# A transformer block with attention and two chosen experts: curve in pieces, row sums in DRAM, maxima turned on VectorE, and another order at both ends

## The chip, the cores and the metric

The kernel runs on one core of a Trainium2 chip. The metric is the device time of one execution in microseconds (us), as the median of several runs; smaller is better. Single instructions are read from one profiled execution.

## The reference

The input x has 4 sequences of 2048 tokens with 512 numbers each, all in float32. The block adds three things:

```python
xn = _layernorm(x, axis=-1)
x = x + attention(xn) + ffn(xn)
# attention: 16 heads of 32; softmax(q k^T / sqrt(32)) v, then a projection with bias
# ffn: per sequence, the first token chooses the 2 best of 8 experts;
#      sum over both of (gelu(xn W1 + b1) W2 + b2), divided by 2
```

The Gelu is the exact one (approximate=False). Each softmax subtracts the row's maximum.

## The kernel before, in words

**Units of work.** `B` is 4 sequences, `DC` 4 groups of 4 heads (a group fills the 128 partitions, 32 for each head), `NCH` 4 chunks of `CH` = 512 queries, `NT` 16 tiles of 128 keys. A unit is one step of one key tile for one chunk and group; there are 4 × 4 × 4 × 16 = 1024, and the loop at L829 goes through them with `U`, beginning `LEAD` = 22 steps early, at U = -22.

**A step.** Attention is done in two passes, and each step does one part of each. The first pass, 22 steps ahead, multiplies queries with keys only to find the maxima (`score_max`, L706, four matmuls m, each reduced by VectorE at L855). The second pass makes the scores again with the keys on the partitions: `shift` (L720) first writes the negated maxima into four PSUM banks s by a bf16 matmul of `ones_b` with `negm`, `score` (L729) adds the products, and ScalarE takes the exponential of each bank into p (L849). On even steps `weigh` (L738) multiplies two p tiles by v, into a ninth bank, acc. All tiles of a step come from one ring of eight PSUM banks (`bank`, L277), in the order in which the code asks for them. p has four buffers.

**The softmax sums.** GpSimd adds the 16 p tiles of a chunk into `psum` (`add_weights`, L756); the last tile is added by an accumulating DMA that GpSimd issues (L764). In the next chunk matmuls with `ones` sum over the keys (`add_keys`, L768, key step 4 or 5), VectorE takes reciprocals in four pieces (L870), GpSimd multiplies (`divide`, L816, key step 12 or 14), and the result goes to DRAM. In the last chunk of all no additions are made on GpSimd: `add_last` (L786) sums pairs of p tiles by matmuls.

**The maxima as shifts.** At the end of a chunk's first pass (key step 9 of the chunk before its own) VectorE reduces to the negated maxima, `neg` (L794). One step on, GpSimd splits them into three bf16 parts (`rest`, L796, casts at L799). Three steps after that `turn_maxima` (L805) transposes the parts by four TensorE transposes (L809) and VectorE copies them to `negm` (L812).

**Dense work.** On odd steps `dense` (L585) takes one item of a plan (`Plan`, L38): projections to q, k and v for the group or sequence to come, the first expert layer (w1, in seven products `STEPS` of block-combined operands, grouped in `GAPS`), the second (w2) or the output projection (proj). `Plan` gives the fixed items their slots, fills the others in order, and leaves some slots empty ("rests", at key step 5); it moves a rest away from the slot in which a curve is due (`curve`, L147). It also says at which step each load is issued: up to eight steps before its first use, in order on SP's queue (`loads`, L218).

**The curve.** Once the product (3, 1) or (2, 1) of a w1 part is in, half of the hidden tile, 128 × 2048, is complete. It is put down for two steps later (`curves`, L625 to L627). There ScalarE applies Gelu at L853, behind the step's four exponentials. In such a step `dense` leaves combining to VectorE. ScalarE's functions live in tables, which an instruction of their own loads: Gelu, exp and the square root each need another.

**Rows.** A w2 item adds its product to a row tile (L633), which goes through `part_dram`. For the first expert the row is loaded from x, and four steps later GpSimd adds the sequence's bias to it (L881): `bias` holds the mean of both experts' b2 plus the projection's bias (`load_bias`, `sum_bias`, L647 to L664).

**Normalisation.** Of the later sequences it is spread over the steps. The square root of all variances (`root`, L431) comes in one step of each of these sequences: VectorE adds epsilon (L433), ScalarE takes the root (L434), VectorE the reciprocal, GpSimd the rest.

**Both ends.** Before the loop the first sequence is normalised, turned and projected chunk by chunk (L666 to L689): statistics, root and normalisation of chunk c + 1 are issued behind the turning of chunk c, then K and Q of chunk c. Ahead of it the routing (L459 to L478) chooses the experts. After the loop (L944 on) come the last weighing and sums, the projection of the last chunk but one (`last2`, L952), three quarters of the last chunk's (`last1`, L960), and the last quarter piece by piece: reciprocal, product, matmul (L967), addition, store.

**Queues.** DMAs are issued by SP in program order, apart from the accumulating ones on GpSimd's. A DMA waits on SP for its data or its buffer, and what stands behind it waits too. `later(u, ...)` puts an issue down for the end of step u.

Of the kernel before, what the change touches and what calls it, by code (L numbers as in the profile page):

```python
# [37 lines left out]
class Plan:  # L38
# [6 lines left out]
    def __init__(self, B, DC, NCH, NT, TPC):  # L45
# [193 lines left out]
def block_kernel(  # L239
# [44 lines left out]
    xn_dram, t_dram, v_dram, att_dram, part_dram, ws_dram = {}, {}, {}, {}, {}, {}  # L284
    for b in range(B):
        for k in range(TOP_K):
            ws_dram[b, k] = tc.dram_tile([P, DC, D], F32, name=f"ws_dram_{b}_{k}")
    wqk_dram = [tc.dram_tile([P, DC, D], F32, name=f"wqk_dram_{n}") for n in range(2)]
    for b in range(B):
        for c in range(NCH):  # L290
            xn_dram[b, c] = tc.dram_tile([P, DC, CH], F32, name=f"xn_dram_{b}_{c}")
            v_dram[b, c] = tc.dram_tile([P, TPC, D], F32, name=f"v_dram_{b}_{c}")
            att_dram[b, c] = tc.dram_tile([P, DC, CH], F32, name=f"att_dram_{b}_{c}")
            t_dram[b, c] = tc.dram_tile([P, DC, CH], F32, name=f"t_dram_{b}_{c}")
            for i in range(TPC):
                part_dram[b, c, i] = tc.dram_tile([P, D], F32, name=f"part_dram_{b}_{c}_{i}")
# [45 lines left out]
    def load(tag, key):  # L342
# [30 lines left out]
        elif tag == "row":  # L373
            b, c, k, i = key
            src = part_dram[b, c, i] if k else x[b, c * CH + i * P : c * CH + (i + 1) * P, :]
# [11 lines left out]
    nc.gpsimd.memset(ones, 1.0)  # L387
    ones_b = const.tile([P, P], BF16, name="ones_b")
    nc.gpsimd.memset(ones_b, 1.0)


    spread = []
# [10 lines left out]
    nc.sync.dma_start(x_first[0], x_rows(0, 0))  # L403
# [27 lines left out]
    def root(mv, sd, nb, a, z, np_=P):  # L431

        nc.vector.tensor_scalar(sd[:np_, a:z], mv[:np_, a:z, 1], EPS, None, ALU.add)  # L433
        nc.scalar.activation(sd[:np_, a:z], sd[:np_, a:z], AF.Sqrt)  # L434
# [147 lines left out]

    outs = {}

    def dense(item, U, on_dve, between):  # L585
# [79 lines left out]


    mv, sd, nb = stat_tiles(0)

    def first_norm(c):
        for i in range(TPC):  # L670
            stats(mv, c * TPC + i, x_first[c][:, i, :])
        root(mv, sd, nb, c * TPC, (c + 1) * TPC)
# [3 lines left out]
    first_norm(0)  # L676
    for c in range(NCH):
# [108 lines left out]
    def add_last(u):  # L786
        add_keys(
            place(u)[:3], bank(f"keys_{u}"), [pT[u], pT[u + 1]], u > plan.units - NT
        )

    def split(where, n):

        neg = small.tile([P, GH, TPC], F32, tag="neg", name="neg_%d_%d_%d" % where)
        nc.vector.tensor_reduce(neg, mx[where], AX.X, ALU.min)  # L794

        def rest():  # L796
            s = spread[n % 2].rearrange("p i j d -> p j i d")
            for part in range(3):
                nc.gpsimd.tensor_copy(s[:, :, :, part], neg)  # L799
                if part < 2:  # L800
                    nc.gpsimd.tensor_tensor(neg, neg, s[:, :, :, part], ALU.subtract)

        return rest

    def turn_maxima(where, n):  # L805
        negm[where] = small.tile([P, CH], BF16, tag="negm", name="negm_%d_%d_%d" % where)
        pt = ps.tile([P, CH], BF16, tag="bank", name="mt_%d_%d_%d" % where)
        for i in range(TPC):
            nc.tensor.transpose(  # L809
                pt[:, ts(i, P)], spread[n % 2][:, i].rearrange("p j d -> p (j d)"), ident_b  # L810
            )
        nc.vector.tensor_copy(negm[where], pt)  # L812
# [6 lines left out]

    loads = plan.loads(BUFS, -LEAD - 1)  # L820
# [6 lines left out]
    row_ready = {}  # L827

    for U in range(-LEAD, plan.units):  # L829
# [21 lines left out]
        if curve is not None:  # L851
            flat = curve.rearrange("p f n -> p (f n)")
            nc.scalar.activation(flat, flat, AF.Gelu)  # L853
        for dst, t in maxima:
# [25 lines left out]
        for t, key in row_ready.pop(U, []):  # L880
            nc.gpsimd.tensor_tensor(t, t, bias[key[0]], ALU.add)  # L881
        if second:
            add_weights(U)

# [10 lines left out]
        for step, sb, n in plan.extra.get(U, []):  # L895
# [6 lines left out]
            elif step == "root":  # L902
                root(*norms[sb], 0, NT)
            elif step == "normal":
# [7 lines left out]
        if last % NT == 3 and NT < last <= plan.units + 3:  # L912
            turn_maxima(*pending[1:3])
# [6 lines left out]
        for s, tag, key in loads.get(U, []):  # L920
            t = load(tag, key)
            if tag == "row" and key[2] == 0:
                row_ready.setdefault(U + 4, []).append((t, key))
# [22 lines left out]
    add_last(U - 2)  # L946
    where = place(U - 1)[:3]
    w = held["wb", ("proj",)]
    for i in range(TPC):
        pp = bank(f"last2_{i}")  # L950
        for g in range(DC):
            nc.tensor.matmul(  # L952
                pp, ends[2][:, g, ts(i, P)], w[:, g, :], start=(g == 0), stop=(g == DC - 1)
            )
        finish(B - 1, NCH - 2, i, pp, ends[3][:, i, :], U)
# [7 lines left out]
    for i in range(TPC):  # L963
        q = ts(i, P)
        nc.vector.reciprocal(sums[where][:, q], sums[where][:, q])  # L965
        nc.vector.tensor_tensor(att[where][:, q], sacc[where][:, q], sums[where][:, q], ALU.mult)  # L966
        nc.tensor.matmul(  # L967
            tail[i], att[where][:, ts(i, P)], w[:, DC - 1, :], start=False, stop=True
        )
# [47 lines left out]
```

## Time and profile before

| What | Value |
|---|---|
| median of 3 runs | 5042.79 us (5037.69 to 5044.59) |
| the profiled execution | 5042.55 us |
| its span in the profile | 5040.8 us |
| mean granted TensorE clock | 0.997 |
| Gelu on 128 × 2048 (L853) | 32 times, 1912 ns |
| exponential on 128 × 512 (L849) | 4096 times, 603 ns |
| addition to psum on GpSimd (L766) | 819 times, 4545 ns |
| mean busy share of the DMA engines | a third, 113 GB/s |

A group's line gives source line, engine, operation, output and inputs, shape, count, then busy time in us, the mean in ns, and the engine's idle time just before it with what ended that. A line of the waits gives who waited, for whom, the total in us, how often and the longest. A timeline's line gives start and length in us, and in brackets the engine's idle time before. PE is TensorE, PEld its weight load, ACT ScalarE, DVE VectorE, POOL GpSimd, SP the engine that issues DMAs. The profiled execution is 1.75 us longer than its span.

### The profile page before, as it was taken

The numbers are of one execution on the slowest core, as the hardware profiler recorded it, in microseconds if no ns is written. First come the engines' busy times: TensorE is split into PE (matmuls) and PEld (weight loads), VectorE is DVE, ScalarE is ACT, GpSimd is POOL, SyncE is SP. The second block draws the span as 40 slices with busy tenths as digits, with TensorE's granted clock in tenths as the row PEclk, the third lists the DMA queues.
The fourth block names the chain that finished last, engine by engine and source line by source line (L and its number), as shares of the span: only waits on it lengthen the run. The fifth ranks groups of instructions, "written<-read, shape, count | busy, mean of one in ns | idle before, by whom it ended". The sixth has DMA issues, their size and how long they took to land. (4 is left out here: it accounts for less than half of the span.)

```text
span 5040.8 us, 107883 instructions
## 1 busy us (share of the span) xinstructions
PE 4947.0 (98%) x45028; PEld 1725.8 (34%) x45028; DVE 3740.2 (74%) x5909; ACT 2394.0 (47%) x4406; POOL 4429.2 (88%) x1498
## 2 busy tenths in 40 slices
PE   8999999999999999999999999999999999999998
PEld 2333333333333333333333333333333333333332
DVE  5777887777777788777777777877777777777762
ACT  1445445454444545454444444555444445454453
POOL 2799998999898998999889998999988988999981
PEclk9999999999999999999999999999999999999999
DMA  6333334433233434434224234434423343323312
GB/s 219 111 103 117 115 96 127 142 122 109 80 107 104 126 107 122 140 114 141 89 86 125 85 121 118 146 122 136 134 70 106 100 123 101 101 80 101 107 62 95
DMA packets 297128, 568.16 MB, mean 113 GB/s; under 512 B 24636, under 2 KB 144188, under 8 KB 279744
## 3 DMA queue, kind: packets, MB, share of 16 engines
q1 hardware_dynamic: 287568, 495.19, 29.4%
q0 software_dynamic: 9072, 66.06, 6.7%
q8 instruction: 354, 5.80, 0.5%
q14 instruction: 134, 1.10, 0.1%
HBM read 367.44 MB, written 127.66 MB: 98 GB/s over the span
## 5 line engine op out<-in xcount | busy, mean ns | idle before, releaser
L766 POOL TENSOR_TENSOR psum<-psum,p 128x2048 f32<-128x2048 f32 x819 | 3722.4, 4545 | 167.6 <-ACT p L849 129.2
L849 ACT ACTIVATE p<-s 128x512 f32<-128x512 f32 x4096 | 2118.0, 603 | 2364.9 <-PE m L715 2181.8
L855 DVE TENSOR_REDUCE mx<-m 128x1 f32<-128x512 f32 x4096 | 2544.2, 684 | 570.1 <-PE m L715 569.8
L733 PE MATMUL s<-qT,kT 32*128 32x512 f32 x8192 | 1919.1, 588 | 0.0
L715 PE MATMUL m<-kT,qT 32*128 32x512 f32 x8192 | 1911.3, 590 | 6.4 <-ACT h L524 3.4
L715 PEld LDWEIGHTS m<-kT,qT 32*128 32x128 f32 x8192 | 920.9, 184 | 334.9 <-issue 244.7
L745 PE MATMUL acc<-p,v 128*32 128x512 f32 x8192 | 988.5, 600 | 37.0 <-ACT p L849 37.0
L733 PEld LDWEIGHTS s<-qT,kT 32*128 32x128 f32 x8192 | 768.6, 185 | 29.2 <-issue 7.3
L485 PE MATMUL ops<-wb_w,h 128*32 128x512 f32 x4096 | 466.0, 595 | 0.6 <-ACT p L849 0.2
L745 PEld LDWEIGHTS acc<-p,v 128*32 128x32 f32 x8192 | 214.2, 109 | 737.0 <-ACT p L849 420.5
L762 POOL TENSOR_TENSOR psum<-p,p 128x2048 f32<-128x2048 f32 x63 | 287.5, 4563 | 203.2 <-ACT p L849 203.2
L754 DVE TENSOR_TENSOR sacc<-acc,sacc 128x512 f32<-128x512 f32 x448 | 309.9, 692 | 158.3 <-PE acc L745 158.3
L485 PE MATMUL hps<-xt,wt_w 128*32 128x512 f32 x3584 | 411.0, 596 | 2.5 <-ACT p L849 2.0
L725 PE MATMUL s<-negm,ones_b 32*128 32x512 bf16 x4096 | 405.7, 385 | 6.2 <-ACT p L849 5.9
L485 PE MATMUL qkps<-xt,wt_qk 128*32 128x512 f32 x3360 | 387.8, 599 | 9.8 <-ACT p L849 9.2
L725 PEld LDWEIGHTS <-ones_b 32*128 32x128 bf16 x4096 | 103.2, 91 | 858.2 <-issue 858.1
L870 DVE RECIPROCAL sums<-sums 128x128 f32<-128x128 f32 x252 | 237.6, 943 | 0.7 <-ACT sums L784 0.7
L485 PEld LDWEIGHTS ops<-wb_w,h 128*32 128x32 f32 x4096 | 120.0, 109 | 308.6 <-issue 229.8
L633 DVE SCALAR_TENSOR_TENSOR row<-ops,row 128x512 f32<-128x512 f32 x128 | 88.4, 691 | 170.3 <-PE ops L485 116.3
L485 PE MATMUL prps<-wb_proj,xl_at 128*32 128x512 f32 x1792 | 203.9, 595 | 0.3
L485 PEld LDWEIGHTS hps<-xt,wt_w 128*32 128x32 f32 x3584 | 103.3, 109 | 268.2 <-issue 186.1
L485 PEld LDWEIGHTS qkps<-xt,wt_qk 128*32 128x32 f32 x3360 | 97.3, 110 | 273.9 <-issue 181.6
(123 smaller groups left out, 1981.6 us busy)
## 6 DMA issues: line engine op xcount, KB each, us to landing
xt<-t_dram SPq DMA_DIRECT2D x181, 512.0 KB, 4.3
xt<-xn_dram SPq DMA_DIRECT2D x133, 512.0 KB, 5.0
psum<-p POOLq DMA_DIRECT2D x63, 1024.0 KB, 8.2
part_dram<-row SPq DMA_DIRECT2D x128, 256.0 KB, 2.0
v_dram<-v SPq DMA_DIRECT2D x64, 256.0 KB, 2.7
wt_w<-ws_dram SPq DMA_DIRECT2D x128, 128.0 KB, 3.3
v<-v_dram SPq DMA_DIRECT2D x64, 256.0 KB, 4.9
row<-in_x_dram SPq DMA_DIRECT2D x64, 256.0 KB, 6.5
```

The costliest lines, as they stand in the source:

```text
L485: nc.tensor.matmul(pp[rows_of(j), :], lhsT[:, rows_of(j)], rhs, start=(first and n == 0), stop=(last and n == len(terms) - 1),)
L633: nc.vector.scalar_tensor_tensor(row, pp, 0.5, row, ALU.mult, ALU.add)
L715: nc.tensor.matmul(t, qT[b, g, qc][r, ts(i, P)], kT[b, g, kc][r, :], start=True, stop=True)
L725: nc.tensor.matmul(tiles[j], ones_b[r, :], negm[b, g, qc][r, :], start=True, stop=False)
L733: nc.tensor.matmul(tiles[j], kT[b, g, kt // TPC][r, ts(kt % TPC, P)], qT[b, g, qc][r, :], start=False, stop=True,)
L745: nc.tensor.matmul(acc[r, :], held["v", (b, g, kt // TPC)][:, (kt + n) % TPC, r], pT[u + n][:, j, :], start=(n == 0), stop=(n == 1),)
L754: nc.vector.tensor_tensor(t, acc, t, ALU.add)
L762: nc.gpsimd.tensor_tensor(psums[b, g, qc], pT[u - 1], pT[u], ALU.add)
L766: nc.gpsimd.tensor_tensor(psums[b, g, qc], psums[b, g, qc], pT[u], ALU.add)
L849: nc.scalar.activation(pT[U][:, j, :], tiles[j], AF.Exp, scale=SCALE)
L855: nc.vector.tensor_reduce(dst, t, AX.X, ALU.max, negate=True)
L870: nc.vector.reciprocal(sums[before][:, q], sums[before][:, q])
```

## The change

Gelu works on halves of 128 × 1024, each in a step of its own, and each is followed by a tiny exponential (`back_to_exp`); a root is, too. `Plan` keeps rests away from all four such slots.

For the sequences after the first, x is copied to `base_dram` by SP (four copies, key steps 6 to 12 of one chunk of group 2 of the sequence before), and at key step 0 of the next chunk GpSimd issues four DMAs that add the bias there. Rows of the first expert are loaded from it; GpSimd's addition at L881 stays for the first sequence alone, behind `add_weights`.

The negated maxima are transposed by VectorE in blocks of 32 × 32. GpSimd splits them as before; at key step 12 SP stores the parts to `parts_dram` in four DMAs, and at 13 fetches them into `negms` in four. TensorE's transposes and VectorE's copy go.

In `root` epsilon is the bias of ScalarE's instruction. The first chunk of x is loaded in four DMAs. At the start the turning of chunk c + 1 is issued between K and Q of chunk c. In the last chunk GpSimd sums some p tiles. At the end `last1` comes first, with all four reciprocals and products ahead of the additions, then `last2`.

```diff
@@ -144,7 +144,10 @@
                 self.items[s] = [fixed.pop(s)]
                 before = None
                 continue
-            curve = before is not None and before[0] == "w1" and before[4][-1] in ((3, 1), (2, 1))
+            curve = before is not None and (
+                before[0] == "w1" and before[4][-1] in ((3, 0), (3, 1), (2, 1))
+                or before[0] == "w2" and before[3] % 2 == 1 and before[5] == 0
+            )
             before = None
             if s in rests:
                 owed += share
...
+                if it[0] == "w2" and it[4] == 0 and it[1]:
+                    self.first_load["row", (it[1], it[3], 0, it[5])] = (
+                        (it[1] - 1) * self.per_seq + 2 * self.per_group + NT + 1
+                    )
...
+    parts_dram = [
+        tc.dram_tile([3, GH * TPC, TPC, HD], BF16, name=f"parts_dram_{n}") for n in range(2)
+    ]
...
+            first_rows = base_dram[b, c][:, i, :] if b else x[b, c * CH + i * P : c * CH + (i + 1) * P, :]
+            src = part_dram[b, c, i] if k else first_rows
...
-    ident_b = const.tile([P, P], BF16, name="ident_b")
-    nc.vector.tensor_copy(ident_b, ident)
+    eps = const.tile([P, 1], F32, name="eps")
+    nc.gpsimd.memset(eps, EPS)
     ones = const.tile([P, HD], F32, name="ones")
     nc.gpsimd.memset(ones, 1.0)
...
     for i in range(2):
-        t = const.tile([P, TPC, GH, HD], BF16, name=f"spread{i}")
+        t = const.tile([P, HD], F32, name=f"negs{i}")
         nc.gpsimd.memset(t, 0.0)
-        spread.append(t)
+        negs.append(t)
+        t = const.tile([P, CH], BF16, name=f"negms{i}")
+        nc.gpsimd.memset(t, 0.0)
+        negms.append(t)
...
-    nc.sync.dma_start(x_first[0], x_rows(0, 0))
+    for i in range(TPC):
+        nc.sync.dma_start(x_first[0][:, i, :], x[0, ts(i, P), :])
...
-        nc.vector.tensor_scalar(sd[:np_, a:z], mv[:np_, a:z, 1], EPS, None, ALU.add)
-        nc.scalar.activation(sd[:np_, a:z], sd[:np_, a:z], AF.Sqrt)
+        nc.scalar.activation(sd[:np_, a:z], mv[:np_, a:z, 1], AF.Sqrt, bias=eps[:np_])
...
-                if (i, q) in ((3, 1), (2, 1)):
-                    at = U + 2 if U > 0 or U == -1 else U + 1
-                    curves[at] = hT[i == 3]
+                if i == 3:
+                    curves[following(U)] = hT[1][:, 2 * q : 2 * q + 2, :]
+                if (i, q) == (2, 1):
+                    curves[following(U)] = hT[0][:, :2, :]
+                    curves[following(following(U))] = hT[0][:, 2:, :]
...
+    def back_to_exp():
+
+        nc.scalar.activation(unused, ones[:, :1], AF.Exp)
+
+    def copy_rows(b, c):
+        nc.sync.dma_start(base_dram[b, c], x_rows(b, c))
+
+    def add_bias(b, c):
+
+        nc.gpsimd.dma_start(
+            base_dram[b, c], bias[b].unsqueeze(1).to_broadcast([P, TPC, D]), accum_op=ALU.add
+        )
...
+
+    first_stats(0)
+    first_norm(0)
+    first_stats(1)
+    first_turn(0)
+    for c in range(NCH):
         if c + 1 < NCH:
             first_norm(c + 1)
-        for kind in "kq":
-            project_qk(kind, 0, 0, c, xn, wkq["kq".index(kind)][:, :, :P])
+        project_qk("k", 0, 0, c, stage[0, c], wkq[0][:, :, :P])
+        if c + 2 < NCH:
+            first_stats(c + 2)
+        if c + 1 < NCH:
+            first_turn(c + 1)
+        project_qk("q", 0, 0, c, stage[0, c], wkq[1][:, :, :P])
...
         b, g, qc, kt = place(u)
-        if kt == 0 or u >= plan.units - NT:
+        if u >= plan.units - NT:
+            if kt == 3:
+                psums[b, g, qc] = pair.tile([P, GH, CH], F32, tag="psum", name="psum_last")
+                nc.gpsimd.tensor_tensor(psums[b, g, qc], pT[u - 1], pT[u], ALU.add)
+            elif kt in (5, 7, 9):
+                nc.gpsimd.tensor_tensor(psums[b, g, qc], psums[b, g, qc], pT[u], ALU.add)
+        elif kt == 0:
             return
-        if kt == 1:
+        elif kt == 1:
             psums[b, g, qc] = pair.tile([P, GH, CH], F32, tag="psum", name=f"psum_{b}_{g}_{qc}")
             nc.gpsimd.tensor_tensor(psums[b, g, qc], pT[u - 1], pT[u], ALU.add)
         elif kt == NT - 1:
...
             nc.scalar.activation(sums[where], ps, AF.Identity)
 
     def add_last(u):
-        add_keys(
-            place(u)[:3], bank(f"keys_{u}"), [pT[u], pT[u + 1]], u > plan.units - NT
+        where, kt = place(u)[:3], place(u)[3]
+        if kt == 2:
+            return
+        weights = [pT[u]] if kt in (4, 6, 8) else [pT[u], pT[u + 1]]
+        if kt == 12:
+            weights.append(psums[where])
+        add_keys(where, bank(f"keys_{u}"), weights, kt > 0)
+
+    def split(where, n):
+
+
+        neg = negs[n % 2]
+        nc.vector.tensor_reduce(
+            neg[:, : GH * TPC].rearrange("p (j i) -> p j i", j=GH), mx[where], AX.X, ALU.min
         )
-
-    def split(where, n):
-
-        neg = small.tile([P, GH, TPC], F32, tag="neg", name="neg_%d_%d_%d" % where)
-        nc.vector.tensor_reduce(neg, mx[where], AX.X, ALU.min)
+        turned = small.tile([P, HD], F32, tag="turned", name="turned_%d_%d_%d" % where)
+        nc.vector.transpose(turned, neg)
+        parts = small.tile([P, 3, HD], BF16, tag="parts", name="parts_%d_%d_%d" % where)
+        negm[where] = negms[n % 2]
 
         def rest():
-            s = spread[n % 2].rearrange("p i j d -> p j i d")
             for part in range(3):
-                nc.gpsimd.tensor_copy(s[:, :, :, part], neg)
+                nc.gpsimd.tensor_copy(parts[:, part], turned)
                 if part < 2:
-                    nc.gpsimd.tensor_tensor(neg, neg, s[:, :, :, part], ALU.subtract)
-
-        return rest
-
-    def turn_maxima(where, n):
-        negm[where] = small.tile([P, CH], BF16, tag="negm", name="negm_%d_%d_%d" % where)
-        pt = ps.tile([P, CH], BF16, tag="bank", name="mt_%d_%d_%d" % where)
-        for i in range(TPC):
-            nc.tensor.transpose(
-                pt[:, ts(i, P)], spread[n % 2][:, i].rearrange("p j d -> p (j d)"), ident_b
-            )
-        nc.vector.tensor_copy(negm[where], pt)
+                    nc.gpsimd.tensor_tensor(turned, turned, parts[:, part], ALU.subtract)
+
+        def store():
+            for t in range(TPC):
+                nc.sync.dma_start(
+                    parts_dram[n % 2][:, :, t, :].rearrange("s r q -> r s q"),
+                    parts[t * HD : t * HD + GH * TPC],
+                )
+
+        def fetch():
+            for j in range(GH):
+                nc.sync.dma_start(
+                    negms[n % 2][j * HD : j * HD + 3, :],
+                    parts_dram[n % 2][:, ts(j, TPC)].rearrange("s i t q -> s (i t q)"),
+                )
+
+        return rest, store, fetch
 
     att = {}
...
             nc.vector.tensor_reduce(dst, t, AX.X, ALU.max, negate=True)
         last = U + LEAD
         if first_pass is not None and last % NT == NT - 1:
             where, n = place(last)[:3], last // NT
-            rest = split(where, n)
-            mark = U
-            pending = (rest, where, n, mark)
+            pending = split(where, n)
+            later(U + 3, pending[1])
+            later(U + 4, pending[2])
         if last % NT == 0 and 0 < last <= plan.units:
             pending[0]()
...
-        for t, key in row_ready.pop(U, []):
-            nc.gpsimd.tensor_tensor(t, t, bias[key[0]], ALU.add)
         if second:
             add_weights(U)
+        for t in row_ready.pop(U, []):
+            nc.gpsimd.tensor_tensor(t, t, bias[0], ALU.add)
 
 
...
+                row_ready.setdefault(U + 4, []).append(t)
         if g == 2 and qc == 0 and kt == 0 and second and b + 1 < B:
             new_bias = load_bias(b + 1)
         if g == 2 and qc == 0 and kt == 5 and second and b + 1 < B:
             sum_bias(*new_bias)
+            for c in range(NCH):
+                later(U + 1 + 2 * c, lambda c=c: copy_rows(b + 1, c))
+        if g == 2 and qc == 1 and kt == 0 and second and b + 1 < B:
+            for c in range(NCH):
+                add_bias(b + 1, c)
 
         for n, c in ((16, NCH - 1), (1, NCH - 2)):
...
+
+    def store_finished():
+        for u in sorted(waiting):
+            for do in waiting.pop(u):
+                do()
+
     where = place(U - 1)[:3]
...
-    for i in range(TPC):
-        pp = bank(f"last2_{i}")
-        for g in range(DC):
-            nc.tensor.matmul(
-                pp, ends[2][:, g, ts(i, P)], w[:, g, :], start=(g == 0), stop=(g == DC - 1)
-            )
-        finish(B - 1, NCH - 2, i, pp, ends[3][:, i, :], U)
...
         q = ts(i, P)
         nc.vector.reciprocal(sums[where][:, q], sums[where][:, q])
         nc.vector.tensor_tensor(att[where][:, q], sacc[where][:, q], sums[where][:, q], ALU.mult)
+    for i in range(TPC):
         nc.tensor.matmul(
             tail[i], att[where][:, ts(i, P)], w[:, DC - 1, :], start=False, stop=True
         )
-        finish(B - 1, NCH - 1, i, tail[i], ends[1][:, i, :], U)
-    for u in sorted(waiting):
-        for do in waiting[u]:
-            do()
+        finish(B - 1, NCH - 1, i, tail[i], ends[1][:, i, :], -LEAD)
+        store_finished()
+    for i in range(TPC):
+        pp = bank(f"last2_{i}")
+        for g in range(DC):
+            nc.tensor.matmul(
+                pp, ends[2][:, g, ts(i, P)], w[:, g, :], start=(g == 0), stop=(g == DC - 1)
+            )
+        finish(B - 1, NCH - 2, i, pp, ends[3][:, i, :], -LEAD)
+        store_finished()
```

More of the change, by code (lines that the diff above doesn't have):

```diff
@@ L281, in rows_of @@
         return slice(j * HD, (j + 1) * HD)
-    xn_dram, t_dram, v_dram, att_dram, part_dram, ws_dram = {}, {}, {}, {}, {}, {}
+    base_dram, xn_dram, t_dram, v_dram, att_dram, part_dram, ws_dram = {}, {}, {}, {}, {}, {}, {}
     for b in range(B):
@@ L293, in block_kernel @@
             att_dram[b, c] = tc.dram_tile([P, DC, CH], F32, name=f"att_dram_{b}_{c}")
+            base_dram[b, c] = tc.dram_tile([P, TPC, D], F32, name=f"base_dram_{b}_{c}")
             t_dram[b, c] = tc.dram_tile([P, DC, CH], F32, name=f"t_dram_{b}_{c}")
@@ L374, in load @@
             b, c, k, i = key
-            src = part_dram[b, c, i] if k else x[b, c * CH + i * P : c * CH + (i + 1) * P, :]
+            first_rows = base_dram[b, c][:, i, :] if b else x[b, c * CH + i * P : c * CH + (i + 1) * P, :]
+            src = part_dram[b, c, i] if k else first_rows
             nc.sync.dma_start(t, src)
@@ L383, in block_kernel @@
     make_identity(nc, ident)
-    ident_b = const.tile([P, P], BF16, name="ident_b")
-    nc.vector.tensor_copy(ident_b, ident)
+    eps = const.tile([P, 1], F32, name="eps")
+    nc.gpsimd.memset(eps, EPS)
     ones = const.tile([P, HD], F32, name="ones")
     nc.gpsimd.memset(ones, 1.0)
+    unused = const.tile([P, 1], F32, name="unused")
     ones_b = const.tile([P, P], BF16, name="ones_b")
     nc.gpsimd.memset(ones_b, 1.0)
-    spread = []
+    negs = []
+    negms = []
     for i in range(2):
-        t = const.tile([P, TPC, GH, HD], BF16, name=f"spread{i}")
+        t = const.tile([P, HD], F32, name=f"negs{i}")
         nc.gpsimd.memset(t, 0.0)
-        spread.append(t)
+        negs.append(t)
+        t = const.tile([P, CH], BF16, name=f"negms{i}")
+        nc.gpsimd.memset(t, 0.0)
+        negms.append(t)
     first = pair.tile([B, D], F32, tag="att", name="first")
@@ L581, in blocks, with following @@
                 later(U + (2 if b == 0 else 4), lambda: nc.sync.dma_start(ws_dram[b, k], raw))
+    def following(U):
+        return U + 2 if U >= -1 else U + 1
     outs = {}
@@ L664, in sum_bias, with first_stats, first_norm @@
         nc.gpsimd.tensor_tensor(t, t, pb, ALU.add)
+    def back_to_exp():
[6 more added lines that the diff above has]
+        )
     mv, sd, nb = stat_tiles(0)
-    def first_norm(c):
+    def first_stats(c):
         for i in range(TPC):
             stats(mv, c * TPC + i, x_first[c][:, i, :])
+    def first_norm(c):
         root(mv, sd, nb, c * TPC, (c + 1) * TPC)
@@ L674, in first_norm, with first_turn @@
             normal(x_first[c][:, i, :], sd, nb, c * TPC + i)
-    first_norm(0)
-    for c in range(NCH):
+    def first_turn(c):
         if c < 2:
@@ L818, in divide @@
         nc.gpsimd.tensor_tensor(att[where], sacc[where], sums[where], ALU.mult)
+    row_ready = {}
     loads = plan.loads(BUFS, -LEAD - 1)
@@ L826, in block_kernel @@
     sum_bias(*load_bias(0))
-    row_ready = {}
     for U in range(-LEAD, plan.units):
@@ L853, in block_kernel @@
             nc.scalar.activation(flat, flat, AF.Gelu)
+            back_to_exp()
         for dst, t in maxima:
@@ L903, in block_kernel @@
                 root(*norms[sb], 0, NT)
+                back_to_exp()
             elif step == "normal":
@@ L911, in block_kernel @@
                     later(U + 1, lambda sb=sb, c=c, xs=xs: nc.sync.dma_start(xn_dram[sb, c], xs))
-        if last % NT == 3 and NT < last <= plan.units + 3:
-            turn_maxima(*pending[1:3])
         for item in plan.items.get(U, []):
@@ L921, in block_kernel @@
             t = load(tag, key)
-            if tag == "row" and key[2] == 0:
-                row_ready.setdefault(U + 4, []).append((t, key))
+            if tag == "row" and key[0] == 0 and key[2] == 0:
+                row_ready.setdefault(U + 4, []).append(t)
         if g == 2 and qc == 0 and kt == 0 and second and b + 1 < B:
```

## The prediction

> **What bounds the kernel now.** I read the page first (its busy shares), then the groups of instructions with shapes kept apart, then TensorE's waits, then three timelines, and last the chain that ended last.
>
> ```profile
> PE 4947.0 (98%) x45028; PEld 1725.8 (34%) x45028; DVE 3740.2 (74%) x5909; ACT 2394.0 (47%) x4406; POOL 4429.2 (88%) x1498
> ```
>
> TensorE is busy for all but 94 us of 5040.8. Its steps in the timeline have a fixed pitch: 3.90 us with four shifts, sixteen score matmuls and the weighing, 5.61 us with 32 dense matmuls in the weighing's place. So the time is the sum of TensorE's work plus its stalls. I summed, over the 1024 steps, what each took above the pitch of its kind: 97 us. A microsecond is won only by taking matmuls away or by ending one of these stalls. GpSimd is next (88%). The groups that the edits touch:
>
> ```profile
> L809 PE MATMUL mt<-ident_b,spread 128*128 128x128 bf16 x256 | 25.4, 221 | 0.0
> L853 ACT ACTIVATE h<-h 128x2048 f32<-128x2048 f32 x32 | 61.2, 1912 | 0.4
> L849 ACT ACT_TABLE_LOAD x35 | 44.9, 1283 | 25.6 <-PE m L715 25.5
> L433 DVE TENSOR_SCALAR sd<-mv 128x16 f32<-128x16 f32 x3 | 13.5, 4491 | 0.0
> L794 DVE TENSOR_REDUCE neg<-mx 128x16 f32<-128x64 f32 x64 | 14.1, 220 | 2.2
> L881 POOL TENSOR_TENSOR row<-row,bias 128x512 f32<-128x512 f32 x64 | 83.8, 1309 | 0.0
> L764 POOL DMA_DIRECT2D psum<-p x63 | 54.6, 866 | 16.2 <-POOL psum L766 15.6 <-ACT p L849 0.6
> ```
>
> TensorE's waits, and one of ScalarE's (total, times, longest):
>
> ```profile
> PE acc L745 <- ACT p L849: 37.0, 35, 1.6
> ```
> ```profile
> ACT p L849 <- DMA psum<-p: 36.3, 9, 7.4
> ```
>
> The 35 waits are the curve: 32 Gelus, in nearly every case 1.16 us. The timeline of ScalarE around one of them, and TensorE's answer:
>
> ```profile
> 169.23 2.07 ACT L849 ACTIVATE p<-s 128x512 f32<-128x512 f32 x4 [1.78 <-PE m L715]
> 171.32 1.28 ACT L853 ACT_TABLE_LOAD   x1
> 172.61 1.91 ACT L853 ACTIVATE h<-h 128x2048 f32<-128x2048 f32 x1
> 174.89 1.28 ACT L849 ACT_TABLE_LOAD   x1 [0.37 <-PE m L715]
> 176.19 2.06 ACT L849 ACTIVATE p<-s 128x512 f32<-128x512 f32 x4
> ```
> ```profile
> 176.84 1.92 PE L745 MATMUL acc<-p,v 128*32 128x512 f32 x16 [1.16 <-ACT p L849]
> ```
>
> The weighing takes the ninth PSUM bank of its step, so it waits for the step's first exponential. The table of exp is loaded only when the scores are there (174.89), 0.37 us after ScalarE was free.
>
> **The change, part by part** (minus is a gain; made against the profiled execution's own 5042.55 us).
>
> *Maxima by VectorE.* 64 groups of four transposes leave TensorE's queue. In the two-pass steps a step with them has a pitch of 6.05 instead of 5.61: 0.44 each, 63 × 0.44 + 0.33 (the one in the lead, between the starts at 140.65 and 140.98) = **−28**. It is work of the bound engine, so nothing hides it. VectorE loses a 0.40 us copy and gets a 32-column transpose. No row shows one. Its nearest is L794, 0.22 us whether GpSimd works or not; from above stands L433, 0.17 us when GpSimd is idle and up to 4.9 us beside it. The Trainium skill (SBUF — State Buffer, "SBUF: two separate sides") says that a VectorE instruction in a two-port mode waits for GpSimd's whole instruction, which is what L433 shows; were the transpose such a one, 63 × about 4.5 us of VectorE would delay the maxima and TensorE's banks. I take 0.22, as the reductions and reciprocals between SBUF tiles never show that wait. GpSimd's three casts and two subtractions stay (0.23 to 0.25 us each).
>
> *The new round trip.* Four stores at key step 12 and four fetches at 13 of the chunk before, both on SP's queue. To the shift at step 0 there are 3.90 + 5.61 + 3.90 + 5.61 = 19.0 us. The casts end 15.2 to 27 us before that shift (median 21.9, from the trace). A transfer lands 2.0 us (part_dram) to 9.4 us (2 KB behind others) after its issue; two of them and eight issues of 0.35 us are 7 to 22 us. So the wait is 0 to 3 us a chunk; I take 0, since the medians of most rows are 2 to 5 us. The fetch waits for the stores' landing, with SP's later loads behind it; those are issued up to eight steps (38 us) ahead, and TensorE's waits name no transfer after the start.
>
> *Curve in pieces.* Two Gelus a part become four of 1024 columns. From the two shapes on ScalarE (512: 603 ns, 2048: 1912 ns) a piece is 1.04 us. Redone on the timeline: exps end 171.30, load to 172.60, piece to 173.65, exp's table to 174.93 (its tiny exponential doesn't wait for scores), that exponential 0.2 to 175.14, first real one 175.74. The weighing could start at 175.61, so about 0.2 us is left; with the restart 0.25. 64 × 0.25 = 16, and some 4 for pieces that meet a normalisation (0.83) or a short step: 20 against 38, **−18**. The Trainium skill speaks against it (ScalarE: Activation LUTs, "Table sets: the hidden batching unit"): do all of one set before switching, at about 2.66 us a switch, 1.28 of load and 1.38 of drain. By that figure a piece would stall 0.25 + 2 × 1.38 = 3.0 us, 64 × 3.0 = 192. The trace has no drain: 0.02 us lies ahead of each load and 0.01 behind. I go by the trace.
>
> *Root.* The row L433 is one VectorE instruction that stood behind GpSimd:
>
> ```profile
> 761.74 4.90 DVE L433 TENSOR_SCALAR sd<-mv 128x16 f32<-128x16 f32 x1
> ```
> ```profile
> 766.67 0.21 ACT L434 ACTIVATE sd<-sd 128x16 f32<-128x16 f32 x1 [3.99 <-DVE sd L433]
> ```
>
> ScalarE's square root waited, the exponentials behind it too: the steps around 129, 385 and 641 are 14 us above their pitch, some 1.5 of it a Gelu's. With epsilon as ScalarE's bias the wait is gone; two tables, root and tiny exponential (3.0 us) are left, less than a piece costs. **−11**.
>
> *Rows summed in DRAM.* GpSimd loses 48 × 1.309 = 63 us and issues 12 accumulating DMAs: 0.87 each as L764, up to four times that as they have rows of 2 KB against 8; 10 to 42 us. They come four together at a chunk's first key step, ahead of the next additions; they wait for SP's copies, the last issued three or four steps before. GpSimd has about 9 us of slack a chunk, p has four buffers. What this can move is the nine waits for the accumulation above, about 24 us of TensorE with the 7 near the end: some are issued 1.3 us earlier now, a burst may cost up to 10. Between −10 and +10 I take **−3**. Copies and additions (25 MB, 13 MB) go beside engines that are a third busy.
>
> *Start.* Turning between K and Q ends three waits of 1.27 us (TensorE for the copied stage). Loading by tiles gains nothing: the statistics stand behind the routing, which waits for wr_sb (7.23 us), after x landed (6.97); three more issues ahead of it may cost 0.3. **−3.5**.
>
> *End.* The chain's last part:
>
> ```profile
> 5000.67 13.93 PE last L952 x32
> 5014.60 10.30 PE last L960 x24
> 5024.90 0.87 PE last L967 x2
> ...
> 5034.87 2.09 PE last L967 x2
> 5036.96 0.02 issue
> 5036.98 0.69 DVE end L644
> ```
>
> In the new order: 24 matmuls (10.3), eight at 0.435 (3.5), 32 (13.9), one addition: the last ends at 5000.67 + 27.7 + 0.7 = 5029.1 instead of 5037.67, −8.6; the reciprocals (4 × 1.24, behind two additions) lie beside the 24. In the last chunk 16 matmul groups for the sums become 12, at 0.86: −3.4; GpSimd's four additions have two steps each. **−12**.
>
> Sum: −28 − 18 − 11 − 3 − 3.5 − 12 = −75.5; 5042.55 − 75.5 = **4967 us**. The median of the runs (5042.79) is 0.24 away, so it holds for that too.
>
> **The rivals.**
> 1. *Maxima late* (slower than before). SP's chain is the new wait: parts, stores, landing, fetches, then the shifts of 63 chunks. For: stores of 64-byte pieces, which no row shows, in a queue where 2 KB took 9.4 us. Against: 19 us for what at medians takes 8 to 12. It outweighs the gain once the mean lateness passes 75.5 / 63 = 1.2 us, a trip of over 20 us; at 3 us late, 63 × 3 = 189: 5156 us.
> 2. *Table loads eat the curve's gain.* If a piece stalls 0.8 us, for instance with the tiny exponential slower or pieces in short steps, 64 × 0.8 = 51: 4998 us.
> 3. *GpSimd sets the pace.* Chunks that also prepare weights or tokens are full; bursts and faster steps bring 15 to 20 us of p waits: 4985 us.
> 4. *Nothing comes of it* (the exp load isn't drawn forward, waits move elsewhere): near 5040.
>
> **How the numbers follow.** Forecast 0.70, by itself 4945 to 4985; rival 2 0.10, rival 3 0.12, rival 1 0.05, rival 4 0.03. The range takes in rivals 2 and 3: 4945 to 4998. The lower end adds to 4967 what pieces without any stall (16) and GpSimd at −10 would give. A difference under 0.2% (10 us) couldn't be told from none. Faster 0.93, within 0.02, slower 0.05.
>
> **What would show it.** Right: TensorE's busy time some 35 us lower; no 6.05 us pitch; 67 or so exp table loads without idle ahead of them; waits of the weighing near 0.2 us, 64 times; steps 129, 385, 641 within a microsecond or two of their pitch; the last chain matmuls to the end. Wrong: TensorE's shifts waiting for a DMA into negms (rival 1), a VectorE transpose of microseconds, or ScalarE's waits for the accumulation above 50 us (rival 3).

## The result, and the profile after

The changed kernel takes 4972.03 us (median of 4 runs, 4967.9 to 4974.97) against 5041.85: a ratio of 0.9864, 95% interval 0.9849 to 0.9879. The forecast was 4967, the range 4945 to 4998. The profiled execution took 4967.9 us, the fastest of the four, and its span is 4966.1.

The busy shares of the page:

```profile
PE 4913.9 (99%) x44740; PEld 1712.0 (34%) x44740; DVE 3714.2 (75%) x5899; ACT 2491.9 (50%) x4570; POOL 4403.5 (89%) x1469
```

TensorE lost 33 us of work and 42 us of idle time; it is even more the bound than before. GpSimd's busy time fell by 26 us, but its share rose. New and changed groups:

```profile
L692 ACT ACT_TABLE_LOAD x67 | 86.0, 1283 | 0.9
L922 ACT ACTIVATE h<-h 128x1024 f32<-128x1024 f32 x64 | 67.7, 1058 | 0.7
L699 POOL DMA_DIRECT2D base_dram<-bias x12 | 15.5, 2358 | 0.0
L857 DVE STREAM_TRANSPOSE turned<-negs 128x32 f32<-128x32 f32 x64 | 13.6, 212 | 2.2
```

The exp table is now loaded with no idle time ahead of it (0.9 us in 67 loads). Before, it was 25.6 us in 35 loads: 14.8 ahead of the very first, which still stands there (14.5 us), and 10.7 ahead of the 29 others that waited. VectorE's transpose takes 0.21 us, 0.215 at most in all 64, so it never waits for GpSimd. Of TensorE's waits, these two answer to those of before, and after them the same wait of ScalarE:

```profile
PE acc L793 <- ACT p L918: 5.5, 17, 0.8
...
PE s L773 <- DMA negms<-parts_dram: 0.3, 1, 0.3
```
```profile
ACT p L918 <- DMA psum<-p: 33.9, 8, 8.4
```

The weighing's waits have shrunk from 37.0 us to 5.5 (the view leaves out the shortest ones; what the curve still costs is in the table below). One shift in 64 chunks waited for the new fetch. The wait for the accumulation has hardly changed in sum. The first Gelu piece of the main loop on ScalarE, and TensorE's weighing behind it:

```profile
164.88 2.06 ACT L918 ACTIVATE p<-s 128x512 f32<-128x512 f32 x4 [1.72 <-PE m L763]
166.96 1.28 ACT L922 ACT_TABLE_LOAD   x1
168.26 1.06 ACT L922 ACTIVATE h<-h 128x1024 f32<-128x1024 f32 x1
169.33 1.28 ACT L692 ACT_TABLE_LOAD   x1
170.63 0.20 ACT L692 ACTIVATE unused<-ones 128x1 f32<-128x1 f32 x1
170.74 2.04 ACT L918 ACTIVATE p<-s 128x512 f32<-128x512 f32 x4
```
```profile
171.37 1.92 PE L793 MATMUL acc<-p,v 128*32 128x512 f32 x16
```

From the end of the exponentials to the first one of the next step nothing is idle: 1.28 + 1.06 + 1.28 + 0.20. The weighing starts 2.16 us behind its step's shift (169.21), where 2.04 is the undisturbed distance. And the end:

```profile
4934.58 10.50 PE last L1033 x24
4945.08 3.43 PE last L1041 x8
4948.51 13.75 PE last L1049 x32
4962.26 0.02 issue
4962.28 0.69 DVE end L668
```

Matmuls run through to the last addition.

The pitch of a step is the shortest time that a step with the same matmuls takes, and its excess is what it takes above that. I summed the excess in both traces and put it down to what held the step (a few steps have two causes):

| us | before | after |
|---|---|---|
| start, up to the first shift | 153.8 | 149.3 |
| curve | 38.8 | 17.2 |
| around the roots | 14.4 | 7.0 |
| behind the accumulating DMA | 23.3 | 22.2 |
| other | 27.2 | 26.1 |
| end, from the last step's shift on | 46.7 | 38.9 |

With TensorE's work in the loop, 31 us less (27.6 for the turned maxima, 3.4 in the last chunk), that makes the 74.7 us between the two spans, within rounding. The median moved by 69.8. A term from one pair of traces is good to a microsecond or two at most: the start, for one, took 148.0 to 152.0 us in the eleven traces with the new order.

**A long stall costs more than its length.** A part of the excess isn't waiting. In the kernel before, TensorE stood idle for 3.45 us around the first root, and the matmuls behind it are slow:

```profile
767.43 2.07 PE L715 MATMUL m<-kT,qT 32*128 32x512 f32 x2 [3.45 <-ACT h L524]
769.42 3.64 PE L745 MATMUL acc<-p,v 128*32 128x512 f32 x16
```

A weighing of sixteen matmuls takes 1.92 us elsewhere. Before, in and after this stretch the profile shows TensorE's busy time (with the number of matmuls), the granted clock, the DMA engines' busy share and GB/s:

```profile
756.00:762.00 6.00, 6.00 (x60) 1.00 1.01 333
767.00:773.00 6.00, 5.57 (x18) 0.50 0.80 219
774.00:780.00 6.00, 6.00 (x60) 1.00 0.26 59
```

The clock is granted at 0.50 from 766.8 to 773.6 us, 6.83 us long. The stall and half of that are 6.9 us, of an excess of 7.23 in this step. In the main loops of the fourteen traces of this document TensorE has 30 stalls of over 3 us (3.17 to 6.06), and each is followed by such a stretch of 3.4 us or more. None of the curve's stalls of about 1.2 us is, where no root is near; stalls of 1.4 to 2.9 us are followed by one in some traces and not in others. In the loop these stretches add up to 20.5 us before (steps 130, 467, 642, 1012) and 10.2 after (467, 1012), so up to 5 us of what the change won is the clock's. At the end, the last 10.7 us before stood at 0.50 (two of the last matmuls took 2.09 us, two at full clock 0.87), and the last 0.6 after.

### The profile page after: what moved, and what is told of

The parts are those of the page before. It is cut to its first block, busy times and chain, and to the rows that moved or that the text cites. A ratio compares the mean times of both kernels' runs of the same rounds, so it can differ in the third digit from the quotient of the medians.

```text
span 4966.1 us, 108027 instructions
## 1 busy us (share of the span) xinstructions
PE 4913.9 (99%) x44740; PEld 1712.0 (34%) x44740; DVE 3714.2 (75%) x5899; ACT 2491.9 (50%) x4570; POOL 4403.5 (89%) x1469
## 4 chain that ended last, share of the span: by engine, by line
PE 83%; ACT 6%; POOL 5%; issue 3%; DMA 2%; DVE 1%; SPq 0%; POOLq 0%; ACTq 0%
PE acc L793 17%; PE s L781 15%; PE m L763 15%; PE qkps L503 6%; PE ops L503 6%; PE hps L503 6%; PE s L773 6%; PE vps L503 5%; POOL psum L820 4%; PE prps L503 4%; ACT p L918 3%; DMA psum<-p 2%; PE keys L826 1%; ACT L692 1%; ACT h L922 1%
## 5 line engine op out<-in xcount | busy, mean ns | idle before, releaser
L773 PE MATMUL s<-negms,ones_b 32*128 32x512 bf16 x4096 | 406.2, 385 | 7.5 <-ACT p L918 7.0
L657 DVE SCALAR_TENSOR_TENSOR row<-ops,row 128x512 f32<-128x512 f32 x128 | 88.5, 691 | 163.9 <-PE ops L503 153.6
```

The lines of the kernel that those rows point to most:

```text
L657: nc.vector.scalar_tensor_tensor(row, pp, 0.5, row, ALU.mult, ALU.add)
L773: nc.tensor.matmul(tiles[j], ones_b[r, :], negm[b, g, qc][r, :], start=True, stop=False)
```

## The experiments

Each kernel is the changed one with an edit, unless another is named; differences are between medians, against 4972.03. The kernel before, run beside each group of them, took 5040.6 to 5041.6 us, and 5037.5 beside the last.

**The tiny exponential left out behind a piece.**

```diff
             nc.scalar.activation(flat, flat, AF.Gelu)
-            back_to_exp()
```

> The changed kernel with the tiny exponential left out behind each Gelu piece (kept behind a root). My theory, that a piece and the tiny exponential only work together: the table load for exp waits for the scores again, as before (174.89 in the old timeline, whatever the length of the Gelu ahead of it), so each of the 64 pieces stalls the weighing by about 1.2 us instead of 0.17: 64 x 1.2 = 79 against 17, +60 us, about 5032. Rival, that shorter pieces alone took the stall away: within 5 us of the changed kernel, 4967 to 4977.

5030.03 us (5028.04 to 5031.28), +58. ScalarE's timeline, and TensorE's wait:

```profile
170.36 1.06 ACT L922 ACTIVATE h<-h 128x1024 f32<-128x1024 f32 x1
172.64 1.28 ACT L918 ACT_TABLE_LOAD   x1 [1.23 <-PE m L763]
```
```profile
PE acc L793 <- ACT p L918: 70.2, 66, 1.2
```

The Gelu is done at 171.42, and exp's table isn't loaded before the scores are there, 1.23 us later. The stall is 1.2 us, as with a whole Gelu, but 64 times. Pieces alone would have eaten most of what the whole change gained. The rival, that shorter pieces alone do it, falls.

**Whole Gelus with the tiny exponential, and the curve all as before.** Both have the old condition, `(i, q) in ((3, 1), (2, 1))` with `hT[i == 3]`, and the old rule for rests; the second also loses the line above.

> The changed kernel with whole Gelus (32 of 128 x 2048, the old rule for rests) but the tiny exponential behind each. Theory: the exp table is in at 174.52 + 1.28 + 0.20 = 176.0 of the old timeline instead of 176.19, a stall of about 1.0 us, 32 times: 33 against 17, +16 us, about 4988. Rival, that the early load alone does the work: no more than 5 us slower.

4990.16 us (4987.33 to 4990.9), +18.

```profile
PE acc L787 <- ACT p L912: 31.1, 32, 1.6
```

> The changed kernel with the curve all as before: whole Gelus, no tiny exponential behind them. Theory: 32 stalls of 1.23 come back, 39 against 17 by the steps' excess over their pitch: +22 us, about 4994. If the pieces' gain was paid for elsewhere (more table loads, rests moved), it is less than 10.

4992.11 us (4991.86 to 4993.5), +20.

```profile
PE acc L787 <- ACT p L912: 37.0, 34, 1.6
```

So neither half works by itself. Early loading with whole Gelus wins 2 us over the old curve: its stalls are still about 1.0 us long (33.3 us of excess in sum, without the step that also has a root). Pieces without early loading are 38 us worse than the old curve. Together they fit ScalarE's work into the time that it has.

**Maxima turned by TensorE.** `split`, `turn_maxima` and the call in the loop as before.

> The changed kernel with the maxima turned by TensorE again (four transposes and VectorE's copy per chunk), without the trip through DRAM. Theory, that the trip is hidden and the gain is TensorE's own work: 63 x 0.44 = +27.5 us less 0.7 for the one chunk whose shift waited for the fetch, about 4999. Rival, that the trip costs as well (SP held up, other loads late): clearly less than +27, say +15.

4991.85 us (4987.94 to 4993.93), +19.8, between theory and rival. Between the traces TensorE's work rises by 26.7 us, but the stalls in the loop fall by 6.4. 1.1 of it is the trip's own (steps 399 and 400). Nearly 4 are small: curve stalls and others of 0.1 to 0.4 us, about half of them in steps right behind the transposes. Another 3 are less waiting for the accumulation (99, 163, 611, 723, 931 and 1012, less what 179, 371 and 467 wait longer). Step 130 goes the other way, by 1.6. So little of the difference is the trip's. I read the rest so: with a slower TensorE the other engines are less often late, and work taken from the bound engine is partly given back as waits for the next one. The sums fit that; no run shows it apart from the trip.

**Epsilon by VectorE.**

```diff
-        nc.scalar.activation(sd[:np_, a:z], mv[:np_, a:z, 1], AF.Sqrt, bias=eps[:np_])
+        nc.vector.tensor_scalar(sd[:np_, a:z], mv[:np_, a:z, 1], EPS, None, ALU.add)
+        nc.scalar.activation(sd[:np_, a:z], sd[:np_, a:z], AF.Sqrt)
```

> The changed kernel with epsilon added by VectorE again ahead of each root. Theory: the steps at 129, 385 and 641 lose what they won, 14.4 against 7.0 us above their pitch, +7, about 4979. If the whole forecast of this part had been right (11), +11. Rival, that the tiny exponential behind the root did the work, not the missing VectorE instruction: within 2 us of the changed kernel.

4980.48 us (4979.45 to 4983.33), +8.5. The groups show the instruction behind GpSimd again, 4.27 us for 16 columns where the 4-column form took 0.16 at the start:

```profile
L452 DVE TENSOR_SCALAR sd<-mv 128x16 f32<-128x16 f32 x3 | 12.8, 4272 | 0.0
```

Steps 130 and 642 are 7.85 and 4.85 us above their pitch instead of 2.19 and 0, and behind both stands a stretch at half clock (6.8 us each), which the changed kernel doesn't have there. So the rival falls: the root's gain is the missing VectorE instruction.

**Row bias by GpSimd.** First rows from x, `tensor_tensor(t, t, bias[key[0]], ALU.add)` ahead of `add_weights`, no copies and no DMAs with `add_bias`.

> The changed kernel with all first rows loaded from x and the bias added by GpSimd again, ahead of its addition to psum; no copies, no accumulating DMAs for the bias. Theory: GpSimd's busy time is 30 to 40 us higher, but it is not the bound; the waits for the accumulation are the same 20 to 25 us, so the time stays within 3 us of the changed kernel, 4969 to 4975. Rival, that GpSimd's relief was a gain: +5 to +10.

4984.44 us (4983.3 to 4988.06), +12.4. My theory falls. ScalarE's wait:

```profile
ACT p L903 <- DMA psum<-p: 52.7, 11, 8.3
```

Waits that were small at the old pace have grown. The excess of step 211 goes from 0 in the changed kernel to 7.18 us (1.04 in the kernel before, which also has the additions), that of 691 from 0.81 to 4.86 (2.13). Ahead of these steps GpSimd issues the accumulating DMA 9.6 and 10.4 us after the next chunk's first shift, against 6.1 and 5.1 in the changed kernel and 7.0 and 8.8 in the kernel before. (It then lands after 11.0 and 8.3 us, in the changed kernel after 8.2 and 10.4, so the landing isn't what the two have in common.) Of the two excesses, 1.7 us each is half clock behind the stall; in this trace the stretches at half clock add up to 27.3 us in the loop, in the changed kernel's to 10.2 us. I formed another theory: GpSimd's relief is worth more at a faster pace. It says that at the old pace the same part brings little. So I gave it to the kernel before, alone:

> The kernel before with the rows' part of the change alone (copies to DRAM, bias added there, GpSimd's 48 additions gone). Undone in the changed kernel this part cost 12 us, by waits for the accumulation that grew (211: 0 to 7.2, 691: 0.8 to 4.9). Theory, that GpSimd's relief is worth more at the changed kernel's faster pace: at the old pace only the waits of the profile before are to be had (1.0, 1.4, 1.9, 1.3 at steps 211, 403, 611, 691): -2 to -6 us, about 5037. Rival, that it is worth 12 at either pace: about 5029.

5037.25 us (5034.96 to 5041.44) against 5041.6, ratio 0.9992 (0.9983 to 1.0001): 4 us by the medians, the size that the new theory gave, not clear of zero by itself, and well short of 12. In its trace the steps 211, 403, 611 and 691 win 5.4 us in sum. So the same part is worth less at the old pace. How much of the 12 is longer waiting, and how much that the waits at 211 and 691 grew past 3 us and brought the slow clock, isn't taken apart. Nor is the order, as the edit also moves the additions back ahead of `add_weights`.

**Both ends as before.** `first_norm` and its loop, one DMA for x, `add_weights`, `add_last` and all behind the loop from the kernel before.

> The changed kernel with both ends as before: x loaded in one DMA, K and Q together behind each turning, last sums by TensorE alone, last2 ahead of last1. Theory from the two traces: start +4.6, last chunk +3.4, tail +7.7 us, together +16, about 4988. A part of that hidden would show as less than +10.

4988.77 us (4981.53 to 4991.72), +16.7. The start gives 4.4 in the trace, the end from the last shift on 7.9, the last chunk 3.4. The start's share is the uncertain one: 153.8, 151.5 and 153.6 us in the three traces with the old start, 148.0 to 152.0 in the eleven with the new, about 3 us between the means.

**The trip two steps later.**

```diff
-            later(U + 3, pending[1])
-            later(U + 4, pending[2])
+            later(U + 5, pending[1])
+            later(U + 6, pending[2])
```

> The changed kernel with stores and fetches of the maxima two steps later (key steps 14 and 15), one step before the shift. Theory: in the changed kernel 15.3 us (median, smallest 0.35) lie between the fetches' issue and the shift; two steps are 9.5 us, a pair of small transfers some 5, so most chunks are still in time and the late ones cost 1 to 3 us: +5 to +25 us. Rival, that the trip has room to spare (SP runs ahead of TensorE): under +3. Rival, that it is as long as I feared (over 10 us): every chunk late, over +60.

5011.4 us (5003.75 to 5023.44), +39, more than the theory's upper end and less than "every chunk late". TensorE's waits in the profiled execution, the fastest of the five:

```profile
PE s L773 <- DMA negms<-parts_dram: 24.0, 7, 5.2
```

Seven shifts wait, up to 5 us; the stalls at the four worst chunks, with the step ahead, are 7 to 10 us each. That is more than the 24.0 us of waits: behind the long ones the clock is at 0.50 again, 41.0 us in this loop against 10.2 in the changed kernel's, so up to 15 us are the clock's. My theory had only the waits. So most chunks could spare two steps, and seven could not. This was the rival that would have made the change slower, and two steps of program order decide more than half of the gain.

**The accumulation, where it is late.** Behind chunks 28 and 62 stand the longest waits. There GpSimd adds the last p tile itself:

```diff
-        elif kt == NT - 1:
+        elif kt == NT - 1 and u // NT not in (28, 62):
```

> The changed kernel, but in chunks 28 and 62, behind which the longest waits for the accumulating DMA stand (7.4 us at step 467, 8.3 at 1012), GpSimd adds the last p tile itself (4.55 us) instead of issuing the DMA (10.2 and 12.1 us to landing). Theory: p is free 5 to 7 us earlier, both waits nearly vanish, -11 us, about 4961. Rival, that GpSimd is so late there that its own addition is as late: within 3 us of the changed kernel.

4959.21 us (4957.7 to 4960.78), −12.8. The two excesses (7.4 and 8.3 us) are gone; at step 468 a new one of 4.2 stands.

> As the one before, in eight chunks (5, 9, 22, 28, 37, 42, 57, 62), behind each of which the profile shows a wait for the accumulation (1.7, 1.1, 1.1, 7.4, 0.6, 0.8, 1.4, 8.3 us). Theory: these go too, -6 more, about 4955. Rival, that the 3.7 us more of GpSimd's time in each of these full chunks comes back as waits behind the next chunk: no better than the one with two.

4955.28 us (4954.58 to 4957.68), −16.8; ratio to the kernel before 0.9831 (0.9818 to 0.9845). The best version. The wait for the accumulation is down to

```profile
ACT p L918 <- DMA psum<-p: 5.3, 2, 3.2
```

and in all chunks:

> The changed kernel with GpSimd adding the last p tile itself in all 63 chunks, no accumulating DMA for the sums. GpSimd works 4.55 instead of 0.87 us there: 63 x 3.7 = 232 us more, 4404 + 232 = 4636 us busy, 93 to 94% of the time. Theory, that the DMA is worth its lateness in most chunks: chunks that also prepare weights or tokens fall behind and p comes late, +10 to +30 on the version with eight, 4965 to 4985. Rival, that the slack of 12% is enough everywhere: 4955 or below.

4971.88 us (4970.81 to 4973.57): the gain of the eight is gone (against the kernel before, beside it, the ratio is 0.9869, the changed kernel's 0.9864). The busy shares and ScalarE's new waits:

```profile
PE 4913.5 (99%) x44740; PEld 1712.2 (34%) x44740; DVE 3715.5 (75%) x5899; ACT 2491.1 (50%) x4570; POOL 4632.0 (93%) x1469
```
```profile
ACT p L918 <- POOL psum L816: 30.4, 6, 6.3
ACT p L918 <- POOL psum L820: 29.3, 11, 3.8
```

With 93% busy GpSimd comes late for ScalarE in 17 places. So the DMA, which takes GpSimd 0.87 us instead of 4.55, pays in most chunks, and costs in those where ScalarE waits for its landing (10.2 and 12.1 us behind chunks 28 and 62).

## Why the prediction was right, point by point

The direction and the sum held: −75.5 forecast, −69.8 measured. The sum was met better than its terms, and that was partly luck. The terms, as the traces show them and as undoing them costs:

| part | forecast | between the traces | undone |
|---|---|---|---|
| maxima by VectorE | −28 | −27.6 work, +1.1 stall | +19.8 |
| curve | −18 | −21.6 | +20 |
| root | −11 | −7.4 | +8.5 |
| rows | −3 | −1.1 | +12.4 |
| both ends | −15.5 | −4.6, −3.4, −7.7 | +16.7 |

The last column adds up to 77.4, more than the change moved, so the parts aren't independent.

*Maxima, round trip.* Right: the transposes' 0.44 us each were TensorE's time. Transpose 0.21 us, forecast 0.22. The trip is hidden but for one chunk: SP issues the fetches 15.3 us ahead of the shift in the median, 0.35 in that chunk. I had reasoned with SP at TensorE's step; it is 2.7 us ahead of it in the median, and in the late chunk a store of part_dram and the parts held it up. That removing this work is worth less than the work itself (19.8 of 27), I had not seen.

*Curve.* Right, with its mechanism: 1.06 us a piece (1.04), 0.20 the tiny exponential, and stalls of 0.17 us in most of 64 steps. Both ScalarE tables cost 1.28 us with 0.02 around them. The Trainium skill (ScalarE: Activation LUTs, "What ACT_TABLE_LOAD costs") states another 1.38 us of drain for every switch. With it the pieces would have been a loss of over 150 us, by the prediction's estimate; no run shows a drain in this sequence.

*Root.* Mechanism right, size off by 3.6 us. The profile shows what is left around the first root:

```profile
752.57 0.31 ACT L452 ACTIVATE sd<-mv,eps 128x16 f32<-128x16 f32 x1
752.90 1.28 ACT L692 ACT_TABLE_LOAD   x1
754.19 0.20 ACT L692 ACTIVATE unused<-ones 128x1 f32<-128x1 f32 x1
```

With the root's own table load ahead, 3.1 us, as I worked out; but "less than a piece costs" held a dense step of 5.61 us to be there. Step 129 has only 16 dense matmuls, 3.90 us, so 2.2 us stand out; in 385 the root meets a Gelu piece, four tables in one step, 3.3 us. So the sign "within a microsecond or two of their pitch" came true at 641 and just about at 129, but not at 385; in six other traces half clock follows there and makes it 4.0 to 5.0 us. Of the 14 us that I counted before, up to 5 were half clock and not waiting; they went with the stalls.

*Rows.* Here the step failed: "what this can move is the nine waits for the accumulation above". That read the worth of GpSimd's relief from waits at the old pace. By itself at that pace it is some 4 us; beside the other edits, which bring TensorE sooner to each p buffer, it holds back 12. Against undoing, the maxima came out 8 us short and the rows 9 us over: I take both for the same oversight, with opposite signs, and that they nearly cancel is luck. The twelve DMAs for the bias kept GpSimd busy for 15.5 us, 1.3 each (the mean of 2.36 us in their line counts the time in which four of them overlap), inside the bounds of 10 and 42. Moving the addition for the first sequence behind `add_weights` has a small price: step 128, 1.5 us waiting for VectorE's row.

*Ends.* Right in sum: −15.7 in the traces, −15.5 forecast. The tail gave 0.9 less than its 8.6; the start gave 1.1 more than its 3.5 in this pair of traces, which is within its scatter. Loading by tiles gained nothing, as worked out: the statistics start at 8.35 us instead of 8.29.

*Rivals.* Table loads eating the gain: excluded. GpSimd as pace-maker: true in part. 22 us of excess stand behind the accumulation, and the version with eight chunks is 16.8 us faster. Maxima late: not here, but two steps off.

What is left open: the "other" excess of 26 us (0.29 us at some thirty steps, 1.3 us at the first ones) is nearly the same before and after, and I didn't look for its cause. How long a stall must be before the clock falls wasn't tried. Which of SP's instructions holds the late trips up was not tried.

## What to carry to other kernels

Where one engine sets the pace in a regular loop, give each kind of step its pitch and read stalls as excess over it; each edit then has its own row in the account. Look at the granted clock behind every long stall, as such a stall can cost more than its length. In this loop a table load stood behind its first user's wait, so a cheap early user drew it forward, and only with it did cutting the function into pieces pay. The worth of relieving the second busiest engine can't be read from its waits at the old pace: work it out for the pace that the other edits bring, and expect that part of what the bound engine wins may show up there.

## What the runs showed of the hardware that I had not expected

A DMA that accumulates a broadcast tile of 1 MB into DRAM took 1.3 us of GpSimd's time, in bursts of four, and 24.1 us to land (median of 12), against 0.87 and 8.6 for 1 MB from p into SBUF. The square root's table load at the very start stood behind the statistics that its first user waits for (3.31 us instead of 0.73) once epsilon became a bias. With epsilon on VectorE again it is back at 0.73, 2.9 us ahead of its user, so a load doesn't always share its user's wait. The routing, which had waited 1.47 us for its weights before, hid the delay. And the granted clock fell to 0.50, for 3.4 to 10.2 us, behind each of the 30 stalls of TensorE over 3 us.
